# Order and engines of the start-up of a fused Swin block and dynamic convolution on one core: zeroing, bias rows, bias tables and late loads

## The chip, the core and the metric

The kernel runs on one core of a Trainium2 chip. The core has five engines that run their own instruction streams in order: TensorE (PE in the profile; its weight loads are PEld), VectorE (DVE), ScalarE (ACT), GpSimd (POOL) and SyncE (SP), which here only issues transfers. Transfers run on 16 shared DMA engines. TensorE reads SBUF and writes PSUM; PSUM is handed out in four pairs of banks, numbered 0 to 3 in the code.

The metric is device time in microseconds of one execution. The kernel before takes 3045.67 us, the median of three runs (3045.51 to 3046.77).

## What is computed

Two layers on an fp32 tensor x of 16 images, 192 channels, 56 by 56 pixels:

```python
# layer 0: shifted-window attention block, windows of 7x7, 6 heads of 32
h = ln(x, norm1_g, norm1_b)              # over channels, per pixel
h = roll(h, (-3, -3)); win = windows(h)  # 64 windows of 49 tokens per image
q, k, v = split(win @ qkv_w + qkv_b);  q = q * SCALE
attn = softmax(q @ k.T + rel_bias_table + mask)
x1 = x + roll_back(attn @ v @ proj_w + proj_b)
y  = gelu(ln(x1, norm2_g, norm2_b) @ fc1_w + fc1_b) @ fc2_w + fc2_b
x2 = x1 + y
# layer 1: 3x3 depthwise convolution whose taps come from the pooled image
t   = relu(batchnorm(mean(x2) @ w1.T));  taps = (t @ w2.T + b2) * causal_mask
out = depthwise_conv(x2, taps) + bias
```

All runs in one launch; the gains of both normalizations are folded into the weights, and their shifts into the biases.

## The kernel before

**Steps.** One step is seven rows of the upper half and the seven rows 28 further down of one image, that is, 16 windows held as two sets of 8; four steps make an image, 64 steps the batch. `images[b]` holds channels 0 to 127 in one tile and channels 128 to 191 of both halves in another.

**Order.** The schedule is written out by hand: what stands in the code is the order in which each engine gets its instructions (`tc.manual_schedule()`), and each engine executes its own in order. Waits come from data and from the reuse of tiles; tiles that share a tag share a buffer. The loop `for i in range(2, NS + 2)` interleaves the MLP of step i-2, the attention of step i, queries and keys of step i+1 and normalization statistics of step i+2. Ahead of it stand some 250 lines that load parameters and carry steps 0 and 1 through the same stages. The change is there only.

**Normalization.** `norm_stats` forms means of x and of x squared by matmuls with `sel` (tiles `st_a`, `st_b`, `st_c`, then `st`). `norm_vars` takes the squares of the means (ScalarE, L349) and subtracts them (VectorE, L350), `norm_root` takes the root (L354), a VectorE reciprocal of 2.6 us follows. `norm_spread` writes the rows to DRAM and reads them back, each copied to all 128 partitions (`rows`, `dv_*`). Only step 0 takes another way: two matmuls with a column of the identity spread its rows into PSUM (`dv_0`). `norm1_scale` multiplies x by them into windows (`win`, L391 and L399), `norm2_scale` into `yn` (L413 and L419).

**Biases.** `shift` multiplies the norm's shift by the raw weights and copies one row out of PSUM to partition 0 (`qkb_row`, `f1b_row`, L190). `turn_row` turns pieces of that row into columns by matmuls with one row and one column each; VectorE adds them to `qkb`, `bv` (L967) and `f1b` (L1051).

**Operands that must be zero.** Keys go block by block into `kbd` and values into `vbd[0]`, `vbd[1]`, probabilities into `prob[0..3]`; the rest of those tiles stays zero. VectorE clears `kbd` (L922), GpSimd clears `vbd` and `prob` (L997).

**Bias tables.** `biases(r, e)` adds the relative bias and the mask into `bias_t`: six VectorE additions a call (L911). Tables with r = 1 are used by the last step of each image only, first by step 3. All four calls stand in one place, ahead of step 0's scores.

**Attention.** `attention_qk` makes queries and keys (`pq`, `pk`, `pe`), `attention_v` values (`pv`), copied out by `attention_v_out` in two blocks, half by VectorE and half by ScalarE (L524), VectorE first. `attention_scores` gives `sc` and closures `top` (maximum, subtraction, exponential) and `share` (sum, reciprocal, and on GpSimd the product into `prob`, L568). `attention_turn` transposes `prob` (`pt`, copied to `prt`), `attention_values` gives `po`, `project` gives `pp`, and `residual` adds it to x (L651, L657).

**Folded statistics.** `norm_folded` adds both row groups and both channel tiles first: `copies` are two transfers (`xs`), `sums` GpSimd additions (L293, L295), `squares` ScalarE or GpSimd squares (L302, L309, L300), and `fold` two GpSimd additions (L314, L315). The loop's first pass needs those of steps 4 (`1_4`) and 1 (`2_1`) for its matmul `st`, which stands in the middle of `mlp_first` (tile `ph`). Just ahead of the loop:

```python
    copies()
    squares(nc.scalar)()
    table(AF.Gelu)
    sums_((0,))
    yns[0] = norm2_scale(0, dvs.pop(1), True)
    sums_((1,))
    fold()
    attention_v_out(pvs)
```

Of the kernel before, what the change touches and what calls it, by code (L numbers as in the profile page):

```python
# [8 lines left out]
F32 = mybir.dt.float32  # L9
AF = mybir.ActivationFunctionType  # L10
ALU = mybir.AluOpType
AX = mybir.AxisListType

DIM, HEADS, HD = 192, 6, 32
# [22 lines left out]
def tile_swin_then_dynamic_conv(  # L37
# [45 lines left out]
    def banks(name, k):  # L83
        return psum.tile([128, 2, 512], F32, tag=f"pair{k}", name=name)

    def mm(dst, lhs, rhs, start, stop):
        nc.tensor.matmul(dst, lhs, rhs, start=start, stop=stop, skip_group_check=True)  # L87
# [33 lines left out]
    def rows2(dst, src, queue):  # L121

        for h in range(2):
            queue.dma_start(dst[h * 64 : h * 64 + 64], src[C0:DIM])

    def columns_load(sources, tag, name, queue):
        n = sum(count for _, count in sources)
        rows = one.tile([n, 256], F32, tag=tag, name=f"{name}_rows")
        at = 0
        for src, count in sources:  # L130
            queue.dma_start(rows[at : at + count, 0:DIM], src.rearrange("(r c) -> r c", c=DIM))
            at += count
        return rows, n, name
# [37 lines left out]
    def fold_center(dst, n, pm):  # L171
        for c in range(2):
            dv = dst[:, c].rearrange("p (c n) -> p c n", c=2)
            nc.vector.tensor_tensor(dv, dv, pm[:, :, : n // 2], ALU.subtract)
# [17 lines left out]

    def turn_row(dst, row, lo, n):
        mm(dst, row[:, lo : lo + n], ident[0:1, 0:1], True, True)

    ident = const.tile([128, 128], F32, tag="ident", name="ident")
# [7 lines left out]
    wqkv = const.tile([128, 2, 3 * DIM], F32, tag="wqkv", name="wqkv")  # L204
    qkb = const.tile([128, 3], F32, tag="qkb", name="qkb")
    wp0 = const.tile([128, DIM], F32, tag="wp0", name="wp0")
    wp1 = const.tile([128, C0], F32, tag="wp1", name="wp1")
    wp2 = const.tile([128, 128], F32, tag="wp2", name="wp2")
    wf1 = const.tile([128, 2, HID], F32, tag="wf1", name="wf1")
    f1b = const.tile([128, NFC], F32, tag="f1b", name="f1b")  # L210
    wf2 = const.tile([128, NFC, DIM], F32, tag="wf2", name="wf2")

# [25 lines left out]
    rel_r = work.tile([PW, N, HEADS], F32, tag="y", name="rel_r", bufs=3)  # L238
    mask_t = one.tile([PW, 2, 2, N], F32, tag="prt", name="mask_t", bufs=4)

# [102 lines left out]

    def norm_vars(keys, st, tag="dev"):

        lo, hi = min(keys) * 32, max(keys) * 32 + 32
        d = one.tile([128, T], F32, tag=tag, name=f"dev_{keys[min(keys)]}")
        part = d[64 + lo : 64 + hi]
        nc.scalar.activation(part, st[lo:hi, 0, :T], AF.Square)  # L349
        nc.vector.tensor_tensor(part, st[64 + lo : 64 + hi, 0, :T], part, ALU.subtract)  # L350
        return part, d
# [4 lines left out]
    def norm_spread(keys, part, tags=("dv1", "sq01"), order=(1, 0)):  # L356

        rows = dram.tile([2 * len(keys), T], F32, tag="rows", name=f"rows_{keys[min(keys)]}")
        nc.sync.dma_start(rows, part[::16])
        out = {}  # L360
        for side in order:
            if side not in keys:
                continue
            v = one.tile([128, 2, T], F32, tag=tags[side], name=f"dv_{keys[side]}")
            at = 2 * (side - min(keys))
            nc.sync.dma_start(
                v,
                rows[at : at + 2].rearrange("(o h) t -> o h t", o=1).broadcast_to([128, 2, T]),
            )
            out[side] = v  # L370
        return out

# [139 lines left out]

    def attention_v_out(pvs):

        for blk, pv in enumerate(pvs):
            src = pv.rearrange("p h (w n) -> p h w n", w=2)[:, :, :, 0:DIM]
            src = src.rearrange("p h w (g j d) -> p h w g j d", j=2, d=HD)
            for h, copy in enumerate((nc.vector.tensor_copy, nc.scalar.copy)):
                for s in range(2):
                    for j in range(2):  # L520
                        dst = vbd[h][j * 64 : j * 64 + N].rearrange(
                            "p (b w s) g (j d) -> p b w s g j d", b=2, s=2, j=2
                        )[:, blk, :, s, :, j, :]
                        copy(dst, src[s * 64 : s * 64 + N, h, :, :, j, :])  # L524
# [351 lines left out]
    load_rows(*images[0], 0, 2 * WS, 3 * WS, nc.sync)  # L876
    load_rows(*images[0], 0, 3 * WS, HALF, nc.sync)
    nc.sync.dma_start(rawf[:, 0], fc1_w[0:C0])
    rows2(rawf[:, 1], fc1_w, nc.sync)
    nc.vector.memset(wp2, 0.0)  # L880
# [7 lines left out]

    nc.sync.dma_start(mask_t, win_mask)

# [14 lines left out]
    def biases(r, e):  # L905
# [15 lines left out]
    g1, be1, bq, bk, bv = columns(*rows1, 2, nc.vector.tensor_copy)  # L921
    nc.vector.memset(kbd, 0.0)  # L922
    norm_squares("1_0", 0, 0, nc.scalar, ("yn0", "q4"))
    fold_scale(
        raw,
# [12 lines left out]
    norm_stats(keys, {0: 0}, st)  # L938
    part, _ = norm_vars(keys, st, "o")
    norm_root(part)  # L940
    nc.vector.reciprocal(part, part)
    norm_squares("1_1", 1, 0, nc.scalar)
    pm = fold_means(wqkv, 3 * DIM, "fq", 0)
    pq = banks("qkb_p", 2)
    row = shift(pq, raw, 3 * DIM, be1, "qkb_row")
    pq = pq[:, 0, 384:390]
    norm_squares("1_2", 2, 1, nc.scalar)

    pd = banks("dv_0", 3)
    for h in range(2):  # L950
        pick_row = ident[64:96, 64 + h * 16 : 65 + h * 16].broadcast_to([32, 128])
        mm(pd[:, h, :T], pick_row, part, True, True)
    fold_center(wqkv, 3 * DIM, pm)
    parts = (
# [7 lines left out]
    for _, c, at, lo, n, _ in parts:  # L962
        turn_row(pq[at : at + n, c : c + 1], row, lo, n)
    g2, be2, f2b, pb, cb = columns(*rows3, 1, nc.scalar.copy)
    norm1_scale(0, pd[:, :, :T], nc.vector)
    for dst, c, at, _, n, b in parts:
        nc.vector.tensor_tensor(dst, b, pq[at : at + n, c : c + 1], ALU.add)  # L967
    nc.vector.tensor_scalar(qkb[:, 0:1], qkb[:, 0:1], SCALE, None, ALU.mult)
    nc.vector.tensor_scalar(qkb[0:64, 2:3], qkb[0:64, 2:3], SCALE, None, ALU.mult)
    nc.vector.tensor_scalar(kb, pick, qkb[:, 1:2], None, ALU.mult)  # L970


    st = banks("st_b", 0)
    keys = {0: "1_1", 1: "1_2"}
    norm_stats(keys, {0: 1, 1: 2}, st)
    part, _ = norm_vars(keys, st)
    norm_root(part)
# [3 lines left out]
    images[1] = load_x(1, nc.sync)  # L981
    for r in range(2):
        for e in range(2):
            biases(r, e)
    nc.gpsimd.dma_start(wp0, proj_w[0:C0])
# [8 lines left out]
    for k, v in enumerate((running_var, running_mean, gamma, beta)):  # L994
        nc.gpsimd.dma_start(bn[:, k], v.rearrange("(o r) -> o r", o=1).broadcast_to([128, RED]))
    for t in (*vbd, *prob):
        nc.gpsimd.memset(t, 0.0)  # L997

# [9 lines left out]
    norm1_scale(1, dvs.pop(0), nc.gpsimd)  # L1008
    w2v = w2.rearrange("(c t) r -> c t r", t=9)[:, 0:NTAP, :]
    b2v = b2.rearrange("(c t) -> c t", t=9)[:, 0:NTAP]  # L1010
    nc.gpsimd.dma_start(w2n[:, 0], w2v[0:C0])
    nc.gpsimd.dma_start(b2t[:, 0], b2v[0:C0])
    rows2(w2n[:, 1], w2v, nc.gpsimd)
    rows2(b2t[:, 1], b2v, nc.gpsimd)
    nc.gpsimd.dma_start(wf2, fc2_w.rearrange("(f p) n -> p f n", p=128))


    top, share = attention_scores(0, *qs.pop(0), (3, 2, 0, 1))
    pv = banks("pb_p", 3)
    pbp, f1p, pt = pv[:, 0, 384:386], pv[:, 0, 392 : 392 + NFC], pv[:, 1, 384:512]  # L1020
    top(0)
    row = shift(pv, rawf, HID, be2, "f1b_row")

    def rows_to_columns():
        for f in range(NFC):
            turn_row(f1p[:, f : f + 1], row, f * 128, 128)

    qs[1], outs = attention_qk(1, 2, 0, 1, rows_to_columns, nc.vector)

# [17 lines left out]
    share(2)  # L1047
    share(3)
    for c in range(2):
        nc.vector.tensor_tensor(pb[c], pb[c], pbp[:, c : c + 1], ALU.add)  # L1050
    nc.vector.tensor_tensor(f1b, f1b, f1p, ALU.add)  # L1051
    nc.vector.tensor_copy(w1t, pt.rearrange("p (k r) -> p k r", k=2)[:, :, 0:RED])
# [4 lines left out]
    outs[2]()  # L1057
    outs[3]()
    o = attention_rows(0, attention_values(0, prts, 3, 2))

# [14 lines left out]
    norm1_scale(2, dvs.pop(1), nc.gpsimd)  # L1075
    pm = fold_means(wf1, HID, "ff", 1)
    top(2)
    residual(0, pp, pair1)
    norm_squares("2_0", 0, 1, nc.scalar)
# [15 lines left out]
    nc.vector.reciprocal(part, part)  # L1095
    dvs.update(norm_spread(keys, part))
    prts = [attention_turn(1, wp, (2, 0)[wp % 2]) for wp in range(4)]
# [7 lines left out]
    v_rest()  # L1105
    v_whole()
    copies, sums_, squares, fold = norm_folded("1_4", 4, 0)
    copies()
    squares(nc.scalar)()
    table(AF.Gelu)  # L1110
    sums_((0,))
    yns[0] = norm2_scale(0, dvs.pop(1), True)
    sums_((1,))
    fold()
    attention_v_out(pvs)
    pp, pair1, p_narrow, p_rest, p_whole = project(1, o, 3, 2)
# [244 lines left out]
```

## Time and profile before

| part | value | from |
|---|---|---|
| median time | 3045.67 us | the three runs |
| span of the profiled execution | 3044.4 us | page |
| first matmul | 4.17 us | order of time |
| first `pq` (step 0) | 22.55 us | order of time |
| first `po` (step 0) | 53.27 us | order of time |
| first `ph` of the loop | 96.45 us | order of time |
| TensorE busy, windows of 20 us from 0 to 100 | 15.83, 18.61, 19.53, 19.14, 17.54 us | windows |
| DMA share and rate, 0 to 20 us | 0.89, 208 GB/s | windows |

A line in order of time has a start, a duration, the engine, the line of the code, the operation, output and inputs without buffer numbers, a shape, and how often it was merged. In square brackets stands the idle time of the engine before it, and what ended it. A line of the windows view has the stretch, its length, the busy time of PE, PEld, DVE, ACT and POOL with the number of instructions, the clock that TensorE was granted as a share of full speed, the busy share of the DMA engines, and GB/s. A group line of the page has the busy time and the share of the span. Ends of matmuls are modelled, so durations of consecutive matmuls overlap somewhat; starts are the better guide.

### The profile page before, as it was taken

To read this page: it belongs to the slowest core of one execution; us is meant where nothing else is said; L and a number is where in the kernel's file an instruction comes from. 1 tells how busy PE (TensorE), PEld (TensorE's weight loads), DVE (VectorE), ACT (ScalarE), POOL (GpSimd) and SP (SyncE) were. 2 spreads that over 40 slices of the span, in tenths; PEclk is the share of its full clock that TensorE was granted. 3 is DMA by queue.
4 is the path that set the end of the run, shared out by engine and by line. 5 is a ranking of instruction groups with operands and counts; after the bars stand their busy time and mean duration, and the time that the engine had idled before them with its cause. 6 is when DMAs were issued, how large, how long until landed. Compare 5 with 4: busy or idle time off the path is not lost.

```text
span 3044.4 us, 62149 instructions
## 1 busy us (share of the span) xinstructions
PE 3022.7 (99%) x25174; PEld 1891.4 (62%) x25174; DVE 2156.3 (71%) x3841; ACT 1948.7 (64%) x3159; POOL 1343.5 (44%) x1269
## 2 busy tenths in 40 slices
PE   9999999999999999999999999999999999999998
PEld 5666666666666666666666666666666666666654
DVE  8656677676686676776866867767767668668664
ACT  4666676666666666766766667667666667666563
POOL 6444534444435445344444444453454444444422
PEclk9999999999999999999999999999999999999999
DMA  4112121111211112121121211212111121211101
GB/s 111 33 31 59 41 75 41 43 60 46 73 38 62 52 44 68 44 72 36 41 67 47 70 36 52 65 41 78 39 47 56 46 73 38 62 52 43 33 30 56
DMA packets 68711, 159.89 MB, mean 53 GB/s; under 512 B 11250, under 2 KB 35288, under 8 KB 66504
## 3 DMA queue, kind: packets, MB, share of 16 engines
q1 hardware_dynamic: 66766, 153.84, 16.7%
q8 instruction: 199, 3.26, 0.4%
q0 software_dynamic: 1360, 1.26, 0.3%
q14 instruction: 88, 0.72, 0.1%
q10 hardware_dynamic: 298, 0.81, 0.1%
HBM read 92.24 MB, written 38.93 MB: 43 GB/s over the span
## 4 chain that ended last, share of the span: by engine, by line
PE 97%; DVE 1%; DMA 1%; POOL 1%; issue 0%; ACT 0%; SPq 0%; POOLq 0%; DVEq 0%; ACTq 0%
PE ph L87 26%; PE pf L87 25%; PE pv L87 8%; PE pp L87 8%; PE po L87 6%; PE pq L87 5%; PE pt L581 5%; PE sc L87 4%; PE pk L87 4%; PE pe L87 4%; PE st L87 2%; PE pc L87 0%; DMA wp<-in_L_conv_proj_w_dram 0%; PE pb_p L87 0%; DVE e L559 0%
## 5 line engine op out<-in xcount | busy, mean ns | idle before, releaser
L87 PE MATMUL pf<-hid,wf 128*128 128x392 f32 (+1 forms) x3072 | 802.6, 493 | 1.5 <-DVE e L552 1.5
L87 PE MATMUL ph<-yn,wf 128*128 128x392 f32 (+1 forms) x3072 | 799.3, 497 | 1.8 <-ACT vbd L524 1.5
L568 POOL TENSOR_TENSOR prob<-e,tot 113x588 f32<-113x588 f32 x256 | 298.3, 1176 | 1098.8 <-DVE tot L567 1098.6
L87 PEld LDWEIGHTS ph<-yn,wf 128*128 128x128 f32 (+1 forms) x3072 | 426.4, 188 | 346.6 <-issue 47.5
L87 PEld LDWEIGHTS pf<-hid,wf 128*128 128x128 f32 (+1 forms) x3072 | 386.2, 164 | 301.3 <-issue 120.2
L524 ACT COPY vbd<-pv 49x192 f32<-49x192 f32 x512 | 160.5, 313 | 575.9 <-DVE vbd L524 571.4
L717 DVE SCALAR_TENSOR_TENSOR x<-pf,cols,x 128x784 f32<-128x784 f32 (+1 forms) x128 | 106.2, 830 | 506.3 <-PE pf L87 447.6
L671 ACT ACTIVATE hid<-ph,f1b 128x784 f32<-128x784 f32 x384 | 337.2, 913 | 133.7 <-PE ph L87 132.2
L781 DVE SCALAR_TENSOR_TENSOR y<-x,wt,y 128x770 f32<-128x770 f32 x282 | 287.7, 1030 | 15.3 <-ACT y L773 7.0
L87 PEld LDWEIGHTS pv<-wqkv,win 64*128 64x128 f32 (+1 forms) x2048 | 255.4, 188 | 31.4 <-issue 1.2
L87 PE MATMUL pv<-wqkv,win 64*128 64x192 f32 (+1 forms) x2048 | 272.5, 325 | 0.3 <-DVE kbd L470 0.3
L559 DVE TENSOR_TENSOR e<-e,top 113x588 f32<-113x588 f32 x256 | 262.3, 1025 | 8.9
L293 POOL TENSOR_TENSOR xs<-x,x 64x392 f32<-64x392 f32 x246 | 249.1, 1013 | 34.4 <-DVE x L657 25.1
L87 PE MATMUL pp<-o,wp 128*128 128x392 f32 (+2 forms) x896 | 251.4, 514 | 0.0
L587 ACT COPY prt<-pt 128x678 f32<-128x678 f32 x256 | 179.2, 727 | 111.6 <-PE pt L581 110.1
L259 ACT ACT_TABLE_LOAD x192 | 246.3, 1283 | 5.3 <-issue 1.8
L562 ACT ACTIVATE e<-e 113x588 f32<-113x588 f32 x256 | 177.1, 692 | 109.7 <-DVE e L559 109.7
L552 DVE TENSOR_TENSOR e<-sc,bias_t 113x588 f32<-113x588 f32 x256 | 179.5, 762 | 60.6 <-PE sc L87 59.5
L415 POOL TENSOR_TENSOR yn<-x,dv 128x784 f32<-128x784 f32 x62 | 115.8, 1867 | 234.0 <-DMA dv<-rows 234.0
L581 PEld LDWEIGHTS pt<-ident,prob 113*128 113x128 f32 x1536 | 165.4, 141 | 64.9 <-issue 35.1
L87 PE MATMUL po<-prt,vbd 128*64 128x49 f32 x6144 | 196.8, 223 | 0.2 <-ACT prt L587 0.2
L87 PEld LDWEIGHTS po<-prt,vbd 128*64 128x64 f32 x6144 | 188.8, 138 | 9.4 <-ACT prt L587 0.5
(186 smaller groups left out, 4429.3 us busy)
## 6 DMA issues: line engine op xcount, KB each, us to landing
dv<-rows SPq DMA_DIRECT2D x127, 392.0 KB
xs<-x SPq DMA_DIRECT2D x246, 98.0 KB
x<-in_x_dram SPq DMA_DIRECT2D x15, 1484.0 KB
out_dram<-y SPq DMA_DIRECT2D x46, 392.0 KB
out_dram<-y SPq DMA_DIRECT2D x48, 196.0 KB
x<-in_x_dram SPq DMA_DIRECT2D x15, 392.0 KB
x<-in_x_dram SPq DMA_DIRECT2D x15, 350.0 KB
out_dram<-y SPq DMA_DIRECT2D x16, 308.0 KB
```

Of the source, the lines that this page charges most:

```text
L87: nc.tensor.matmul(dst, lhs, rhs, start=start, stop=stop, skip_group_check=True)
L259: nc.scalar.activation(junk, eps_t[0:1], func)
L293: nc.gpsimd.tensor_tensor(xs[p, 0], v0[p, h], v1[p], ALU.add)
L524: copy(dst, src[s * 64 : s * 64 + N, h, :, :, j, :])
L552: nc.vector.tensor_tensor(e, sc[:PW, :, : HEADS * N], rel, ALU.add)
L559: nc.vector.tensor_tensor(ehs[wp], ehs[wp], t.broadcast_to([PW, 2 * HEADS, N]), ALU.subtract)
L562: nc.scalar.activation(es[wp], es[wp], AF.Exp)
L568: nc.gpsimd.tensor_tensor(prob[wp][:PW, :, 0:N], ehs[wp], t.broadcast_to([PW, 2 * HEADS, N]), ALU.mult)
L581: nc.tensor.transpose(pt[:, a, g * PW : (g + 1) * PW], prob[wp][:PW, h : h + 2, :].rearrange("p h k -> p (h k)"), ident[:PW, :PW],)
L587: nc.scalar.copy(prt, pt[:, :, : 3 * PW])
L671: nc.scalar.activation(hid[:, f], phs[f][:, :, :T], AF.Gelu, bias=f1b[:, f : f + 1])
L781: nc.vector.scalar_tensor_tensor(dst, src, wt[:, kc, t : t + 1], dst, ALU.mult, ALU.add)
```

## The change

- The first step's deviations `d0` become a whole tile of 128 rows, zero but for its 32 rows, and both matmuls of `dv_0` run over all 128 rows instead of 32.
- Rows are turned into columns by transfers: six from `qkb_row` into a new tile `pq`, six from `f1b_row` into `f1p`. `turn_row` goes. The second call of `columns` and its TensorE transposes move behind `st_b`.
- A helper `clear` writes zeros by a ScalarE ACTIVATE with scale 0; `kbd` and both `vbd` are cleared so. `prob` is cleared by GpSimd later, behind the second `norm1_scale`.
- Of the bias tables only those with r = 0 are made at the old place; `biases(1, 0)` and `biases(1, 1)` go behind the key copies of steps 1 and 2.
- The loads of `fc1_w` and of x from row 21 on are issued behind the six transfers, the mask ahead of them and into another tag; the loads of `w2`, `b2` and `fc2_w` on GpSimd's queue go behind the first products into `prob`.
- `residual(0)` stands ahead of `top(2)`. The last spread before the loop is read in two parts, the second behind the `xs` copies. The value copies of step 2 are split around `norm2_scale`, and the squares that are left (`rest`) follow them.

It is meant to take small matmuls and waits out of TensorE's way at the start, and to spread the zeroing and the late tables over engines and stretches with room.

```diff
+    def clear(t):
+        names = "abcd"[: len(t.shape) - 1]
+        flat = t.rearrange(f"p {' '.join(names)} -> p ({' '.join(names)})")
+        nc.scalar.activation(flat, ones[:, 0:1].broadcast_to(flat.shape), AF.Copy, scale=0.0)
...
-    def turn_row(dst, row, lo, n):
-        mm(dst, row[:, lo : lo + n], ident[0:1, 0:1], True, True)
...
-    load_rows(*images[0], 0, 3 * WS, HALF, nc.sync)
-    nc.sync.dma_start(rawf[:, 0], fc1_w[0:C0])
-    rows2(rawf[:, 1], fc1_w, nc.sync)
+    nc.sync.dma_start(mask_t, win_mask)
...
-    nc.vector.memset(kbd, 0.0)
+    d0 = one.tile([128, T], F32, tag="o", name="dev_0")
+    nc.vector.memset(d0, 0.0)
     norm_squares("1_0", 0, 0, nc.scalar, ("yn0", "q4"))
+    clear(kbd)
...
-    part, _ = norm_vars(keys, st, "o")
+    part, _ = norm_vars(keys, st, d0)
+    clear(vbd[0])
     norm_root(part)
...
     norm_squares("1_2", 2, 1, nc.scalar)
+    row = shift(banks("qkb_p", 2), raw, 3 * DIM, be1, "qkb_row")
...
-        turn_row(pq[at : at + n, c : c + 1], row, lo, n)
+        nc.sync.dma_start(pq[at : at + n, c : c + 1], row[:, lo : lo + n])
+    nc.sync.dma_start(rawf[:, 0], fc1_w[0:C0])
+    rows2(rawf[:, 1], fc1_w, nc.sync)
+    load_rows(*images[0], 0, 3 * WS, HALF, nc.sync)
...
-        pick_row = ident[64:96, 64 + h * 16 : 65 + h * 16].broadcast_to([32, 128])
-        mm(pd[:, h, :T], pick_row, part, True, True)
+        pick_row = ident[:, 64 + h * 16 : 65 + h * 16].broadcast_to([128, 128])
+        mm(pd[:, h, :T], pick_row, d0, True, True)
     fold_center(wqkv, 3 * DIM, pm)
+    clear(vbd[1])
...
-    for r in range(2):
-        for e in range(2):
-            biases(r, e)
+    for e in range(2):
+        biases(0, e)
...
-    for t in (*vbd, *prob):
-        nc.gpsimd.memset(t, 0.0)
...
+    for t in prob:
+        nc.gpsimd.memset(t, 0.0)
...
-    def rows_to_columns():
-        for f in range(NFC):
-            turn_row(f1p[:, f : f + 1], row, f * 128, 128)
-
-    qs[1], outs = attention_qk(1, 2, 0, 1, rows_to_columns, nc.vector)
+    for f in range(NFC):
+        nc.sync.dma_start(f1p[:, f : f + 1], row[:, f * 128 : (f + 1) * 128])
+    qs[1], outs = attention_qk(1, 2, 0, 1, None, nc.vector)
...
+    biases(1, 0)
+    nc.vector.tensor_tensor(f1b, f1b, f1p, ALU.add)
...
+    residual(0, pp, pair1)
     top(2)
-    residual(0, pp, pair1)
...
-    dvs.update(norm_spread(keys, part))
+    read = norm_spread(keys, part, order=None)
+    dvs[1] = read(1)
...
+    biases(1, 1)
     copies, sums_, squares, fold = norm_folded("1_4", 4, 0)
     copies()
-    squares(nc.scalar)()
+    rest = squares(nc.scalar)
+    sums_((0,))
+    attention_v_out(pvs, (0,))
+    yns[0] = norm2_scale(0, dvs.pop(1), True)
+    dvs[0] = read(0)
+    attention_v_out(pvs, (1,))
+    rest()
     table(AF.Gelu)
-    sums_((0,))
-    yns[0] = norm2_scale(0, dvs.pop(1), True)
     sums_((1,))
     fold()
-    attention_v_out(pvs)
```

## The prediction

> **What bounds the kernel now.** I read the page's busy shares and its chain, then the table by stages, then the order of time of the first 110 us.
>
> ```profile
> PE 3022.7 (99%) x25174; PEld 1891.4 (62%) x25174; DVE 2156.3 (71%) x3841; ACT 1948.7 (64%) x3159; POOL 1343.5 (44%) x1269
> PE 97%; DVE 1%; DMA 1%; POOL 1%; issue 0%; ACT 0%; SPq 0%; POOLq 0%; DVEq 0%; ACTq 0%
> ```
> TensorE is busy 99% of the span and is 97% of the chain. The table of windows (span, then busy time of PE, PEld, DVE, ACT, POOL, granted clock) says where the rest lies:
> ```profile
> 100.00:3020.00 2920.00, 2916.52 (x24349) 1827.64 (x24349) 2062.20 (x3637) 1890.67 (x3057) 1277.46 (x1169) 1.00 0.17 51
> ```
> Between 100 and 3020 us it idles 3.5 us. The change touches only code that runs before 105 us; the order of instructions in the loop is the same. So everything is decided by when TensorE reaches the loop, and by its idle time before 100 us: 9.4 us (the five windows of 20 us have 15.83, 18.61, 19.53, 19.14 and 17.54 busy), 4.2 of which precede its first matmul.
> ```profile
> 17.00:17.50 0.50, 0.50 (x6) 0.43 (x5) 0.27 (x1) 0.46 (x2) 0.50 (x2) 0.60 1.15 218
> 18.50:19.00 0.50, 0.50 (x5) 0.17 (x8) 0.47 (x2) 0.17 (x1) 0.50 (x2) 0.50 0.82 141
> 24.00:24.50 0.50, 0.50 (x6) 0.35 (x4) 0.02 (x1) 0.48 (x2) 0.50 (x1) 1.00 0.54 25
> ```
> The clock column falls to half from 17.4 to 23.9 us. The order of time (start, duration) of that stretch and of the entry to the loop:
> ```profile
> 16.68 1.55 PE L87 MATMUL qkb_p<-ident,qkb_row 1*128 1x1 f32 x9
> 17.23 0.94 DVE L391 TENSOR_TENSOR win<-x,dv 128x343 f32<-128x343 f32 x2 [1.23 <-PE dv L87]
> 19.95 0.38 DVE L399 TENSOR_TENSOR win<-x,dv 64x21 f32<-64x21 f32 x2
> 22.55 1.59 PE L87 MATMUL pq<-win,wqkv 64*128 64x392 f32 x4
> 43.17 1.49 PE L87 MATMUL pb_p<-ident,f1b_row 1*128 1x1 f32 x12
> ...
> 91.00 1.39 POOL L413 TENSOR_TENSOR yn<-x,dv 128x392 f32<-128x392 f32 x1 [10.93 <-DMA dv<-rows]
> 92.66 1.05 ACT L309 ACTIVATE sq<-x 64x392 f32<-64x392 f32 x2
> 94.74 1.01 POOL L314 TENSOR_TENSOR sq<-sq,sq 128x392 f32<-128x392 f32 x1
> 96.45 8.37 PE L87 MATMUL ph<-yn,wf 128*128 128x392 f32 x36 [1.53 <-ACT vbd L524]
> 103.33 1.18 POOL L315 TENSOR_TENSOR sq<-sq 128x392 f32<-128x392 f32 x1
> 104.75 0.11 PEld L87 LDWEIGHTS st<-xs,sel 128*32 128x32 f32 x2 [0.56 <-POOL sq L315]
> ```
> Two waits matter at the end: ph waits 1.5 us for the value copies, and the loop's first st waits for GpSimd's folds, which are done only 0.2 us before it.
>
> [...] half clock after the 1-row matmuls, and again at 3027.4 to 3031 after a pause. [...] on SyncE's queue the trace has 1.7 us (rows issued at 27.11, its reader at 28.82).
>
> **The change part by part.**
> (1) Zeroing. kbd leaves VectorE (2.02 us), d0 comes (392 elements, about 0.35). VectorE gains nothing: its next work waits for qkv_w until 8.79. [...] vbd[0] (1.5 us) starts at 10.56 and holds the root, due 11.21, until 12.0. The reciprocal (2.6) then ends near 15.25 instead of 14.45; dv is queued behind the qkb_p products until 15.54: free, with 0.3 us left. vbd[1] stands behind qkb_row (16.28) and ends at 17.75, before ScalarE's next input. On GpSimd 2.7 us of vbd memsets go; the prob memsets (2.8) move behind the second norm1_scale.
> (2) dv over 128 rows: the same four instructions by 0.33 us. Row count does not lengthen them (fq_m's matmuls on 64 and on 128 rows both come 0.34 apart); [...] I take the clock as kept, and the other end, the full 6.5 us at half rate, for the range.
> (3) Turned rows. The 12 one-row matmuls and the later cols_p leave the way to st_b, which starts near 17.0, not 18.47: 1.5 us. At full clock st_b takes the 2.2 us of st_c (72.17 to 74.3), not 4.1, and ends at 19.2. Then pq waits for win, whose last row starts at 19.95: pq at 20.4 for 22.55 is 2.15 us, and its short part at full clock (2.2 for 2.8, from 111.87 and from 22.55) 0.65 more: **2.8 us** at the first pv. In place of the matmuls VectorE waits for six transfers. They are issued from 16.3, at 0.53 each (rows) until 19.5, landing 1.7 to 2.5 us later: 21.2 to 22. Behind that wait stand qkb, the scales, the second reciprocal (to 25.1), rows and dv_1. q is wanted at 24.2, dv_1 at 30.8: rows lands by 27 and dv_1 about 3 us after its issue, near 30.3. I take it as hidden; 2.5 us a transfer more would show as 1 us.
> (4) Loads. fc1_w (768 KB) and x from row 21 (588 KB) go behind the six transfers. They land near 26; the first reader wants them at 34.
> (5) Bias tables: 6 additions of 0.236 us each are 1.4 us a table. Two leave the stretch before the first vbd copies, which waited for them (32.80, pv ready at 32.4): 0.4 us. One fits into VectorE's 2.6 us wait at 57.1, one into its 3.6 us at 90.9: free. Now 3.2 us ahead.
> (6) The 12 f1b matmuls (43.17 to 44.6) go: 1.4 us, of which ScalarE's kbd ahead of the first prt keeps some 0.8: **3.8 us** ahead. The f1p transfers queue behind image 1, whose traffic ended at 43 and now starts 2 us earlier; they are wanted at 51.
> (7) residual ahead of top(2). ScalarE's e_2 exponential (0.69) now stands ahead of the squares for st_c, which end 0.4 us after pq: 3.4 us ahead at the third pv.
> (8) Last order. dv_0 is read alone, the second dv after the xs copies; dv_0 lands about 4 us after issue (128.28 to 132.19), near 86. VectorE: first vbd half from 86.4 (pv ready 89.7 less 3.4) 1.5, yn 1.4, second half 1.5: 90.9. ScalarE's half 1.3: 92.2, ahead of ph, which starts when pp is done, 94.9-3.4 = 91.5: 4.9 us ahead. But rest() is now behind both copies: squares 0.53+1.05 end at 93.9. GpSimd's chain, two folds, square, sums, add, square, two folds, took 94.74 to 104.51 with 0.5 of wait: 9.3 us. It now starts at 93.9 and ends at 103.2, or 103.9 if norm1_scale on VectorE slows it, as it did the last two folds (1.29, 1.18 for 1.01). TensorE, at st by 99.8, waits 3.5 to 4 us. st starts near 103.5, against 104.75: **1.2 us is kept of 4.9**.
> Sum: 3045.67 - 1.2 = **3044.5**. A pause this long can cost the clock: one window at half rate is 3.4/2 = 1.7 us, which would turn the case into +0.5.
>
> **Rivals.**
> (a) The lead is kept: if GpSimd's folds start earlier than reckoned (copies without waits, TensorE further ahead), all 4.9 us come through, st's 0.3 us too: 3045.67-5.0 = 3040.7. For it: every step before (8) shortens TensorE's own path. Against it: GpSimd executes in order and its folds need ScalarE's last squares.
> (b) Slower: the clock falls at 17 us anyway (st_b then takes 4.1 us and 1.7 us of the lead are lost) or the six transfers hold dv_1 up, and the pause at st still costs 1.7 us of clock: -1.2+1.7+1.7 = +2.2, so 3047.8. For it: 3027 us shows such a fall after a pause of 4 us.
> (c) Much faster, over 6.1 us: all idle time before 96 us gone, with the clock never cold: 5.2 idle + 3.0 matmuls + 3.2 clock = 11.4 at the very most; 3037 if two thirds of it came. The win chain at 17.23 to 20.33 and GpSimd's chain speak against it.
> (d) Much slower: single-word transfers that take 10 us more than reckoned. VectorE's second reciprocal, rows and dv_1 would move by 10, less the 0.5 us of slack at dv_1, and the lead of 1.2 is gone too: 3045.67+9.5-1.2 = 3054.0. Single words on GpSimd's queue (f1b, 3 KB) landed in 5.4 us here; against.
>
> **How the numbers follow.** Main case 0.50, of it a third with a cold window; (a) 0.27; (b) 0.12; (c) 0.07; (d) 0.04. The range must leave out (c), (d) and the outer half of (b), and hold (a): 3040.2 to 3047.5. 0.2% is 6.1 us: only (c) and (d) pass it; with 0.02 and 0.01 more for errors of the working, faster is 0.09, slower 0.05, and 0.86 lies between.
>
> **What would show it.** st_b starting at 17.0 and lasting 2.2 us, clock column 1.00 from 17 to 24; pq at 20.4; pv's sc near 30.6 (33.83 before); po near 49.5 (53.27); ph near 91.5 to 92 without a wait on vbd; then the first st waiting 3 us or more for GpSimd's L315-type fold, at 103 to 104; possibly a half clock behind it. It is wrong if that st starts before 101 (then (a)), if the clock is half at 18 us, or if qkb's additions wait beyond 23 us. A total under 3039.6 or over 3051.8 would mean that something in the loop changed, which I hold to be untouched.

## The result, and the profile after

The kernel after takes **3054.37 us** (median of 6 runs, 3050.24 to 3059.86) against 3045.59 us before (6 runs, 3044.54 to 3047.28): the ratio is 1.003, with an interval of 1.0017 to 1.0043. It is slower by about 9 us, outside the range of 3040.2 to 3047.5. A second set of 18 runs of the same code (`e1_again` below) gave 3051.55 against 3046.24, ratio 1.002 [1.0013, 1.0027]. The profiled execution was the fastest of the first six: its span is 3048.4 us, 4.0 more than before. (A span leaves out about 1.8 us of the device time: this execution took 3050.24 us, the profiled one of before 3046.2.) So two things have to be found: 4 us that the trace holds, and 1 to 5 us that most executions lose on top of it.

The page of the kernel after, the two lines that answer to those of before (busy shares, chain by engine):

```profile
PE 3021.4 (99%) x25150; PEld 1889.3 (62%) x25150; DVE 2160.2 (71%) x3841; ACT 1952.5 (64%) x3162; POOL 1341.1 (44%) x1267
PE 97%; DVE 1%; POOL 1%; DMA 0%; issue 0%; SPq 0%; ACT 0%; POOLq 0%; DVEq 0%
```

They look the same, though TensorE has 24 matmuls and 1.3 us of work less: averages over 3 ms don't show 4 us. The windows do (stretch, length, busy PE, PEld, DVE, ACT, POOL, granted clock):

```profile
17.00:17.50 0.50, 0.50 (x12) 0.26 (x8) 0.50 (x2) 0.27 (x1) 0.50 (x2) 1.00 0.39 66
18.50:19.00 0.50, 0.50 (x9) 0.20 (x2) 0.47 (x4) 0.00 (x0) 0.50 (x2) 1.00 0.06 2
24.00:24.50 0.50, 0.50 (x3) 0.30 (x2) 0.50 (x1) 0.50 (x1) 0.00 (x0) 1.00 1.28 168
100.00:3020.00 2920.00, 2913.37 (x24319) 1824.88 (x24316) 2063.68 (x3631) 1888.39 (x3055) 1278.70 (x1171) 1.00 0.17 51
107.00:110.00 3.00, 3.00 (x5) 1.18 (x4) 0.57 (x1) 0.49 (x1) 0.00 (x0) 0.50 0.00 0
```

The half clock at 17 to 24 us is gone, as intended. In its place stands one from 106.8 to 110.2 us, just behind a pause of TensorE. A stretch at half clock is called cold below, and in the recorded texts also a cold or half-clock window.

The order of time of the first 40 us of the kernel after (start, duration, engine and line; SPq is SyncE's queue of transfers):

```profile
15.91 3.75 SPq L963 DMA_DIRECT2D pq<-qkb_row  x6
16.84 0.94 DVE L398 TENSOR_TENSOR win<-x,dv 128x343 f32<-128x343 f32 x2 [0.83 <-PE dv L87]
19.88 1.04 PE L87 MATMUL pq<-win,wqkv 64*128 64x392 f32 x4 [0.82 <-ACT dev L355]
21.63 0.15 DVE L983 TENSOR_TENSOR cols<-cols,pq 64x1 f32<-64x1 f32 x1 [0.49 <-DMA pq<-qkb_row]
22.07 2.60 DVE L989 RECIPROCAL dev<-dev 64x392 f32<-64x392 f32 x1
22.76 1.71 SPq L112 DMA_DIRECT2D x<-in_x_dram  x1
24.51 1.36 SPq L113 DMA_DIRECT2D x<-in_x_dram  x1
27.49 0.60 SPq L365 DMA_DIRECT2D rows<-dev  x1
29.86 0.80 SPq L370 DMA_DIRECT2D dv<-rows  x2
33.60 1.82 POOL L398 TENSOR_TENSOR win<-x,dv 128x343 f32<-128x343 f32 x2 [12.07 <-DMA dv<-rows]
39.98 1.23 PE L87 MATMUL pq<-win,wqkv 64*128 64x392 f32 x4 [2.08 <-POOL win L406]
```

The first `pq` starts at 19.88 for 22.55, 2.7 us ahead, and the bias additions wait only until 21.63. But the second reciprocal is done at 24.67 and its `rows` transfer is issued at 27.49: SyncE is still issuing loads of x, two of which hold it for 1.71 and 1.36 us. `dv_1` lands at 33.60, GpSimd needs 6.6 us for step 1's windows, and step 1's `pq` waits 2.08 us. It starts at 39.98; before, 40.37. Of a lead of 3.4 us over the trace of before, 0.4 is left.

The entry to the loop of the kernel after, in order of time:

```profile
85.06 0.92 PE L87 MATMUL pv<-wqkv,win 64*128 64x192 f32 x8
88.75 1.46 DVE L532 COPY vbd<-pv 49x192 f32<-49x192 f32 x4 [1.00 <-PE pv L87]
93.69 1.32 ACT L532 COPY vbd<-pv 49x192 f32<-49x192 f32 x4 [2.04 <-DVE vbd L532]
93.69 8.43 PE L87 MATMUL ph<-yn,wf 128*128 128x392 f32 x36
95.47 1.05 ACT L314 ACTIVATE sq<-x 64x392 f32<-64x392 f32 x2
96.60 1.03 POOL L319 TENSOR_TENSOR sq<-sq,sq 128x392 f32<-128x392 f32 x1 [4.92 <-ACT sq L314]
103.39 0.52 PE L87 MATMUL st<-xs,sel 128*32 128x392 f32 x1 [0.50 <-POOL xs L300]
105.50 1.03 POOL L320 TENSOR_TENSOR sq<-sq 128x392 f32<-128x392 f32 x1
106.59 1.38 PE L87 MATMUL st<-sq,sel 128*32 128x392 f32 x2 [2.35 <-POOL sq L320]
113.16 2.24 PE L87 MATMUL sc<-kbd,q 64*64 64x98 f32 x96
```

Two of these points in the kernel before:

```profile
86.14 0.92 PE L87 MATMUL pv<-wqkv,win 64*128 64x192 f32 x8
109.70 2.24 PE L87 MATMUL sc<-kbd,q 64*64 64x98 f32 x96
```

`ph` starts at 93.69 without a wait, 2.8 us earlier than before. Then GpSimd idles 4.92 us for ScalarE's squares, which stand behind both halves of the value copies; its chain of additions and squares runs from 96.60 to 106.53; TensorE waits 0.50 us for the sum `xs`, then 2.35 us, until 106.59, for the last fold, and the clock falls. Step 2's `sc` starts at 113.16 for 109.70: **3.46 us late**. From there to the end only 0.5 us more is lost; the loop carries a lateness on with little added over 2900 us (4.28 us at the tail's first `pc`, 3031.56 for 3027.28).

### The profile page after: what moved, and what is told of

It is laid out like the page before. It is cut to its first block, busy times and chain, and to the rows that moved or that the text cites. A ratio compares the mean times of both kernels' runs of the same rounds, so it can differ in the third digit from the quotient of the medians.

```text
span 3048.4 us, 62116 instructions
## 1 busy us (share of the span) xinstructions
PE 3021.4 (99%) x25150; PEld 1889.3 (62%) x25150; DVE 2160.2 (71%) x3841; ACT 1952.5 (64%) x3162; POOL 1341.1 (44%) x1267
## 4 chain that ended last, share of the span: by engine, by line
PE 97%; DVE 1%; POOL 1%; DMA 0%; issue 0%; SPq 0%; ACT 0%; POOLq 0%; DVEq 0%
PE ph L87 25%; PE pf L87 25%; PE pv L87 8%; PE pp L87 8%; PE po L87 6%; PE pq L87 5%; PE pt L589 5%; PE sc L87 4%; PE pk L87 4%; PE pe L87 4%; PE st L87 2%; PE pc L87 0%; POOL win L406 0%; DVE e L567 0%; POOL win L398 0%
## 5 line engine op out<-in xcount | busy, mean ns | idle before, releaser
L298 POOL TENSOR_TENSOR xs<-x,x 64x392 f32<-64x392 f32 x246 | 249.5, 1014 | 34.5 <-DVE x L665 25.3
```

What stands on the lines that cost most here:

```text
L298: nc.gpsimd.tensor_tensor(xs[p, 0], v0[p, h], v1[p], ALU.add)
```

## The experiments

**Again, and the two suspects taken away.** Four kernels shared one chip and 54 runs of before (3046.24 us). `e1_again` is the kernel after, unchanged.

> The changed kernel once more, for its spread and a second trace. Its six times so far run from 3050.2 to 3059.9 while the kernel before stays within 3044.5 to 3047.3, and the mean granted clock goes down with the time (0.999 at 3048.4 us of span, 0.996 at 3058.1). Theory A (pauses of TensorE before the loop let the clock fall[...]): again 3050 to 3060; in a slow execution the stretches at half clock lie between 17 and 125 us and at the tail, the loop from 140 to 3000 us has its 1.00. Rival B (something in the loop itself got slower, by another layout of SBUF or other transfer lanes): in a slow execution the loss is spread over the loop, each step of about 46 us longer by 0.1 us or more. Rival C (the loop falls to half clock in places): the half-clock stretches lie inside 140 to 3000 us.

Measured: 3051.55 us, 18 runs from 3049.18 to 3057.29. Its profile repeats the pause at the loop's `st`, and has a half clock at a place where the first profile of the same code had none (order of time, then windows):

```profile
39.23 1.98 PE L87 MATMUL pq<-win,wqkv 64*128 64x392 f32 x4 [1.32 <-POOL win L406]
106.32 0.85 PE L87 MATMUL st<-sq,sel 128*32 128x392 f32 x2 [2.35 <-POOL sq L320]
```
```profile
39.00:42.00 3.00, 2.77 (x8) 2.72 (x10) 2.90 (x7) 1.12 (x2) 2.87 (x6) 0.50 0.85 177
107.50:110.50 3.00, 3.00 (x6) 1.42 (x6) 0.57 (x1) 0.62 (x2) 0.00 (x0) 0.50 0.00 0
```

A pause of 1.32 us went with a cold stretch here (from 38.91 us); one of 2.08 us at the same place did not in the first profile. Apart from these two stretches and one behind the pause at the tail, the clock record of this profile, which begins at 8.2 us, has no half clock before the last matmul, so none inside the loop, as theory A has it. None of the longest executions was profiled. But the granted clock of each execution is on record: in the two sets of the kernel after, the seven executions with a mean clock of 0.999 took 3049.18 to 3050.41 us and the three with 0.996 took 3056.43 to 3059.86. A clock lower by 0.003 over 3050 us is an estimated 9.2 us, as far as three decimals tell; that is the size of the scatter. A loop that got slower at full clock (rival B) would not show in that column.

`e2_squares_first` puts the squares ahead of the value copies, and keeps the rest of the change:

```diff
     copies()
-    rest = squares(nc.scalar)
+    squares(nc.scalar)()
...
     attention_v_out(pvs, (1,))
-    rest()
```

> Changed kernel with one part of step 8 undone: the squares of step 4's folded statistics stand ahead of both value copies again, everything else as changed. Theory A (GpSimd's folds wait for ScalarE's last squares, which stand behind the second value copy; TensorE waits at the loop's first st): in the changed kernel's trace the squares end at 96.5 and the chain of folds takes 10.1 us from 96.6. Here the squares can run when the xs copies land, near 88 to 90, and end near 91; GpSimd starts its folds at its own 91.7 and ends near 101.5; TensorE, at st by 101.9, waits less than 0.5 us; no clock fall there. About 3.5 us for the wait and 1.5 us for the clock less: 3045 or less in its fastest execution, and a spread as small as that of the kernel before if this pause causes the spread. Rival B (another GpSimd or VectorE wait takes its place, residual or the transfers of 2_1): st still starts after 104, at most 1.5 us gained.

Measured: 3045.57 us, ratio 0.9997 [0.9989, 1.0005]. One moved statement is worth 6.0 us (3051.55 less 3045.57), and takes the whole loss away. What is left of the change, steps (1) to (7) of the prediction and the rest of (8), is not told apart from before. In order of time:

```profile
89.73 1.05 ACT L314 ACTIVATE sq<-x 64x392 f32<-64x392 f32 x2
92.15 1.33 POOL L319 TENSOR_TENSOR sq<-sq,sq 128x392 f32<-128x392 f32 x1
101.57 1.17 POOL L320 TENSOR_TENSOR sq<-sq 128x392 f32<-128x392 f32 x1
102.54 0.53 PE L87 MATMUL st<-xs,sel 128*32 128x392 f32 x2
```

The squares end at 90.8 instead of 96.5, GpSimd's last fold at 102.74, and `st` no longer waits.

`e3_x_later` issues x from row 21 on behind the spread of step 1's deviations, so that SyncE is free for `rows`:

```diff
-    load_rows(*images[0], 0, 3 * WS, HALF, nc.sync)
...
     dvs.update(norm_spread(keys, part, tags=("dv1", "yn0"), order=(0, 1)))
+    load_rows(*images[0], 0, 3 * WS, HALF, nc.sync)
     images[1] = load_x(1, nc.sync)
```

> Changed kernel with one load moved: x from row 21 on is issued behind rows and the two dv reads instead of ahead of them. Theory A (SyncE is still issuing that load when the reciprocal is done at 24.7, so rows goes out at 27.5 and dv_1 lands at 33.6; GpSimd's windows and with them TensorE's second pq wait 2.1 us): rows goes out near 24.8, dv_1 lands near 30.5, the second pq starts near 37.9 instead of 39.98, and po of step 0 near 49.5 instead of 51.1. Since the wait at st follows ScalarE and VectorE, which follow TensorE, st also comes about 1.5 us earlier: 1 to 2 us less in all. Rival B (dv_1 is late because of the transfers' own traffic, fc1_w and image 1, not because of the issue order): rows earlier but dv_1 still near 33, no gain.

Measured: 3051.67 us, ratio 1.0017 [1.001, 1.0024], the same as `e1_again`. In order of time:

```profile
30.92 1.82 POOL L398 TENSOR_TENSOR win<-x,dv 128x343 f32<-128x343 f32 x2 [9.54 <-DMA dv<-rows]
37.23 1.00 PE L87 MATMUL pq<-win,wqkv 64*128 64x392 f32 x4
67.94 1.79 PE L87 MATMUL pq<-win,wqkv 64*128 64x392 f32 x4 [1.01 <-POOL win L406]
```
```profile
68.00:72.00 4.00, 4.00 (x20) 1.33 (x24) 3.93 (x7) 1.74 (x3) 1.37 (x2) 0.57 0.00 0
```

The cause of the first wait is shown: with the loads out of the way `dv_1` lands at 30.92 for 33.60 and `pq` of step 1 starts at 37.23 without a wait. The forecast of 1 to 2 us in all fails, as the gain does not last. Step 2's `pq` now comes early enough to wait 1.01 us for GpSimd's `win`, the clock falls behind it in this execution, and the pause at the loop's `st` (106.23, again 2.35 us) is there in any case.

`e4_both` joins the two edits.

> Both edits of the two runs before together. Theory A (the two waits are the whole of the loss): second pq near 37.9, ph near 91 to 92, st without a long wait near 100; about 3041, under the kernel before by 4 to 5 us, with a small spread. Rival B (one of the waits hid another): over 3044. Rival C (the spread is not due to pauses): the time scatters by 5 us and more as that of the changed kernel does.

Measured: 3045.40 us, ratio 0.9996 [0.9988, 1.0004]; not told apart from before, nor from `e2_squares_first`. Theory A's 3041 is missed by over 4 us, and rival B's "over 3044" holds: the two waits are not all. In its profile step 3's first `pq` starts 2.9 us earlier than before (108.99 for 111.87), but the span is only 0.7 us shorter: 0.9 of the lead goes in the loop and 1.3 in the last 100 us.

**The order alone, and the pause filled.** The next four shared a chip and 65 runs of before (3046.77 us). `e5_order_alone` is the kernel before with step 8 of the prediction and nothing else:

```diff
...
-    dvs.update(norm_spread(keys, part))
+    read = norm_spread(keys, part, order=None)
+    dvs[1] = read(1)
...
-    squares(nc.scalar)()
-    table(AF.Gelu)
+    rest = squares(nc.scalar)
     sums_((0,))
+    attention_v_out(pvs, (0,))
     yns[0] = norm2_scale(0, dvs.pop(1), True)
+    dvs[0] = read(0)
+    attention_v_out(pvs, (1,))
+    rest()
+    table(AF.Gelu)
     sums_((1,))
     fold()
-    attention_v_out(pvs)
```

> The kernel before with the last step's order alone (own squares behind both value copies, dv_0 read apart). Theory A, the wait at the loop's first st is the loss: pv ready 89.7, VectorE's half copy to 91.2, yn 92.6, second half 94.1, ScalarE's half 95.4, squares end 96.9, GpSimd's chain 9.9 us, so st's last part at 106.8 instead of 104.75; with one half-clock window behind it the first pq of step 3 at 115.5 instead of 111.9, and the time 3049.5 to 3050.5 against 3046. Theory B, the loss comes from the early part (load order, pauses at 40 us): this order gains the 1 us of ph's wait and the time is 3045 to 3046.

Measured: 3052.34 us, ratio 1.0015 [1.0009, 1.0022]: +5.6 us, where the whole change gave +5.3 in `e1_again`. The order is sufficient by itself. That is 2 us more than theory A's 3049.5 to 3050.5; the cold stretch behind the pause lasts 6.83 us here, two times 3.41. In order of time, with the lines as the kernel before numbers them (its L309, L314 and L315 are L314, L319 and L320 above), and the windows:

```profile
95.05 1.05 ACT L309 ACTIVATE sq<-x 64x392 f32<-64x392 f32 x2
96.18 1.03 POOL L314 TENSOR_TENSOR sq<-sq,sq 128x392 f32<-128x392 f32 x1 [3.62 <-ACT sq L309]
106.17 1.51 PE L87 MATMUL st<-sq,sel 128*32 128x392 f32 x2 [2.35 <-POOL sq L315]
```
```profile
17.00:17.50 0.50, 0.50 (x8) 0.36 (x6) 0.20 (x1) 0.50 (x2) 0.50 (x2) 1.00 1.14 227
100.00:120.00 20.00, 17.15 (x145) 8.52 (x142) 12.01 (x20) 8.65 (x12) 5.88 (x6) 0.83 0.05 11
```

The second fence holds a surprise: this kernel has the one-row matmuls and the 32-row `dv` of before, and its clock at 17 us is full. The fall in the profile of before (at 17.10 us by the clock record; the prediction read 17.4) is not in every execution. That changes how the lead has to be read, since up to 82 us this kernel does what before does (each column is one execution):

| | before | `e5_order_alone` | after |
|---|---|---|---|
| cold at 17 us | 6.83 us | none | none |
| start of the first `pq` | 22.55 | 20.34 | 19.88 |
| start of step 0's `sc` | 33.83 | 31.15 | 30.61 |
| start of step 0's `po` | 53.27 | 51.50 | 51.13 |
| start of step 2's `pv` | 86.14 | 84.34 | 85.06 |

At the first `pq` 2.2 of the 2.7 us that the kernel after gains over the trace of before are gained by the old code as well when its clock stays full, and at step 2's `pv` the kernel after is 0.72 us behind it.

`e6_fill_st` is the kernel after with three extra products ahead of the last `st` product:

```diff
         for k, at in order:
+            if folded and at == 3 and "1_4" in keys.values():
+                for _ in range(3):
+                    mm(st[:, 1, :T], ident, wqkv[:, 0, 0:T], True, True)
```

> The kernel after, with three extra products of 128x392 (about 0.70 us each) put into the unused second bank of the loop's first st tile ahead of its last product; nothing reads them. They fill 2.1 of the 2.4 us that TensorE waits there. Theory A, wait and clock are two separate losses: last st product still near 106.5, granted clock 1.00 from 100 to 120 us, first pq of step 3 near 113.5 (115.1 in the kernel after, 111.9 before), profiled span near 3046.8, and the median falls from 3051.5 by 1.7 (one window) to 3.4 (two windows). Theory B, the slower executions lose their clock elsewhere: the median stays within 1 us of 3051.

Measured: 3050.76 us, ratio 1.0011 [1.0005, 1.0018], +4.0 against its runs of before where `e1_again` had +5.3. The profile:

```profile
105.87 2.24 PE L87 MATMUL st<-wqkv,ident 128*128 128x392 f32 x6
108.29 0.84 PE L87 MATMUL st<-sq,sel 128*32 128x392 f32 x2 [0.19 <-POOL sq L320]
```
```profile
106.50:110.00 3.50, 3.31 (x10) 1.36 (x9) 2.41 (x7) 0.49 (x1) 1.66 (x2) 1.00 0.10 23
```

The clock holds behind `st`, as theory A has it; its other numbers fail. This execution was cold at 39.5 us and once more at 70.2, and so came to 108.29 late, and the median lies within 1 us of 3051, which was theory B's number, not 1.7 to 3.4 us lower. The 1.3 us between the two differences is too small for its intervals to settle. So the trace shows that the pause need not cost the clock, and the median gives no sign that this pause alone makes the slower executions.

`e7_narrow_dv` is `e4_both` with `dv` on 32 rows:

```diff
-        pick_row = ident[:, 64 + h * 16 : 65 + h * 16].broadcast_to([128, 128])
-        mm(pd[:, h, :T], pick_row, d0, True, True)
+        pick_row = ident[64:96, 64 + h * 16 : 65 + h * 16].broadcast_to([32, 128])
+        mm(pd[:, h, :T], pick_row, part, True, True)
```

> e4_both with the first deviations again on 32 rows (dv's products contract over 32 rows). Theory A, the small number of rows is what let the clock fall at 17 us before: half clock from 16 to 20.5 us or to 24, st_b 3.5 to 4 us long instead of 2.1, first sc at 32 to 33 instead of 30.8, time 1.7 us above e4_both: near 3047. Theory B, the one-row products were the reason, and they are gone here: clock 1.00 at 17 us, first sc at 30.8, time equal to e4_both: 3045.4.

Measured: 3045.50 us, ratio 0.9994 [0.9986, 1.0002], as `e4_both`; clock 1.00 from 17 to 18 us, first `sc` at 30.77 (30.83 in `e4_both`). Theory B's numbers; the zeroed 128-row tile did nothing that can be measured. That the one-row products were the reason does not follow: `e5_order_alone` has them too, and its clock held. One trace can't exclude that the clock would fall here in other executions.

**The pauses filled everywhere.** `e8_fills` is `e4_both` with extra products ahead of step 1's and step 2's `pq` and ahead of the tail's first `pc`, where TensorE waits 3.09 us for GpSimd in before and after alike:

```diff
+        if i in (1, 2):
+            mm(ps[0][:, 0, :T], ident, wqkv[:, 0, 0:T], True, True)
         for m in (0, 2, 1):
             short(dsts[m], wqkv, slice(m * 128, (m + 1) * 128), r1, True)
...
         pc = banks(f"pc_{n}", k)
+        for _ in range(0 if n else 4):
+            mm(pc[:, 0, :T], ident, wqkv[:, 0, 0:T], True, True)
```

> e4_both with extra products that nothing reads (128x392, 0.70 us each): one ahead of the first pq of steps 1 and 2, four ahead of the first pc at the tail, each in a bank that is overwritten next. Theory A, half-clock windows follow from pauses: no half window at 40, 70 or behind pc; pc's 32 products take about 10.7 us instead of 12.4, profiled span near 3042, median 3042.5 to 3043.5. Theory B, the pauses do not set the clock: half windows stay, and the time is 3045.4 or a little above.

Measured: **3043.61 us**, ratio 0.9989 [0.9982, 0.9995]: faster than both kernels, and 0.1 above theory A's range. Its clock has no half stretch from 10.8 us until behind its last matmul. Its tail, and below it that of the kernel after:

```profile
3021.16 2.87 PE L87 MATMUL pc<-wqkv,ident 128*128 128x392 f32 x8
3024.42 10.66 PE L87 MATMUL pc<-x,dg 128*128 128x392 f32 x32 [0.40 <-POOL dg L1287]
```
```profile
3031.56 12.35 PE L87 MATMUL pc<-x,dg 128*128 128x392 f32 x32 [3.09 <-POOL dg L1284]
```

The 32 products of `pc` take 10.66 us for 12.35: 2.9 us of work for nothing buys 1.7 us.

`e9_before_tail` is the kernel before with the four products ahead of `pc` alone, `e10_after_fills` the kernel after with its waits left in and filled: two products at step 1's `pq`, one at step 2's, three at `st`, four at `pc`. They shared 25 runs of before (3046.24 us).

> The kernel before with the four extra products of 128x392 ahead of the first pc alone (they fill the 3.1 us pause at the tail; nothing reads them). If the cold window behind that pause costs what e8_fills showed (pc 10.66 us long instead of 12.4 to 13.2, which is 1.7 to 2.5 us), the median falls from 3046.5 to 3044 to 3045, and what e8_fills keeps beyond this (3043.6) is what the mended change is worth: 0.5 to 1.5 us. If the gain of e8_fills came from the early part, this stays at 3046 to 3046.5.

Measured: 3044.69 us, ratio 0.9996 [0.9987, 1.0004]; its profile has `pc` at 10.66 us, and was cold for 3.41 us from 17.44 on. By the medians about half of what `e8_fills` gained is the tail; the rest, some 1.6 us against before (3.16 less 1.55), is what the mended change and the two small fills are worth, and the intervals overlap.

> The kernel after with extra products that nothing reads at each pause: two ahead of pq of step 1, one ahead of pq of step 2, three ahead of the last st product at the loop's entry, four ahead of the first pc. Its waits stay. Theory A, the slower executions of the kernel after (up to 8 us above its fastest) are cold windows behind these pauses: clock 1.00 throughout, last st still near 106.5, median 3046 to 3047.5, and the runs lie within 4 us. Theory B, the clock falls elsewhere too: median 3049 or more, and the runs spread over 6 us or more as before.

Measured: 3047.67 us, ratio 1.0005 [0.9997, 1.0013], 13 runs from 3046.61 to 3049.05: a spread of 2.4 us, where the 18 runs of `e1_again` have 8.1. The waits are where they were, and the clock is full from its first record, at 7.8 us, on; before that the view counts as full what is not recorded, though equal products take longer there (up to 0.86 us in `st_a`, 0.49 to 0.52 in `st_b`, in the kernel after). In order of time, then windows:

```profile
106.60 0.84 PE L87 MATMUL st<-sq,sel 128*32 128x392 f32 x2 [0.18 <-POOL sq L320]
111.52 2.24 PE L87 MATMUL sc<-kbd,q 64*64 64x98 f32 x96
```
```profile
0.00:110.00 110.00, 99.95 (x806) 59.73 (x807) 90.08 (x199) 60.56 (x102) 65.40 (x98) 1.00 0.36 90
110.00:3020.00 2910.00, 2906.21 (x24295) 1822.56 (x24294) 2055.31 (x3619) 1885.46 (x3051) 1272.27 (x1165) 1.00 0.17 51
```

Its last `st` starts at 106.60 as in the kernel after (106.59), and step 2's `sc` at 111.52, not 113.16. So of the 3.46 us there, 1.64 are clock and 1.82 are what the wait costs beyond the lead. And its median lies 1.43 us above before, not 5.3 to 8.8: the slower executions of the kernel after were cold stretches behind pauses. The fill at the tail helps before as well: against `e9_before_tail`, which has it too, the median is 2.98 us longer. The median is 0.2 us above the interval that theory A gave; its other numbers hold.

## Why the prediction was wrong

The steps up to the first scores hold within 0.6 us. Zeroing on ScalarE (1) cost nothing (2.15 us for `kbd`, 1.48 for each `vbd`); `st_b` started at 16.67 (17.0 forecast) and took 2.1 us at full clock (2.2); `pq` at 19.88 (20.4), step 0's `sc` at 30.61 (30.6), the six transfers landed by 21.6 (21.2 to 22), 2.0 us behind the end of their issue. That the whole tile would keep the clock (2) was the author's estimate; no run shows it, and in `e7_narrow_dv` the clock is 1.00 from 17 to 18 us with 32 rows. What loses the time is the order of step (8), by `e2_squares_first` and `e5_order_alone`; the forecast missed it by three wrong terms and by the clock.

**Steps (3) and (4): "I take it as hidden".** `dv_1` was put near 30.3 and landed at 33.60. The transfers of single words were sized rightly, and so was `rows` as far as the reciprocal goes (24.67 for 25.1). What was missed is SyncE's queue itself. Step (4) asked when the loads' bytes land, not how long their issue holds the queue: from 19.7 to 27.0 us. `e3_x_later` shows it: there `rows` is issued at 24.57 in place of 27.49. The lead at the third `pv` (step 2's), put at 3.4 us, measured 1.08 (85.06 for 86.14).

**Step (5), a small one.** Six additions for one table were put at 1.4 us; they took 2.75 at 52.36, beside GpSimd's squares, and step 1's last scores started at 57.52 after 0.82 us of idle time for which the profile names no releaser ("issue"). `e5_order_alone`, which has the tables at the old place, has no stop there: all 96 products of that `sc` in one run of 2.61 us from 54.43. Part of the 1.2 us that the lead shrank between step 0's `po` (51.13 for 53.27) and step 1's `pv` (57.83 for 58.78) is this; it was not tried by itself.

**Step (8): the term mis-sized, the mechanism right.** The wait was named: the squares behind both copies, GpSimd's chain, TensorE stopping at `st`. From values ready to the last `st` the prediction had 17.2 us (86.3 to 103.5), the trace 17.8 (88.75 to 106.59); the chain took 9.9 us for 9.3, stretched where it ran beside VectorE's `win` (L298 2.53 us; 2.09 in `e2_squares_first`, where it ran at 95.80 and `win` began at 99.43). The tables show the like from the other side: the second one's six additions took 1.48 us at 86.27, beside an idle GpSimd, where the first took 2.75. So 2.3 us of the 3.1 at `st` are the lead that was not there, and 0.6 the chain.

The error in reasoning is to have set the lead against the wait. By the prediction's own numbers and with no lead, the last `st` comes at 89.7 + 17.2 = 106.9, 2.2 us behind the 104.75 of before; the lead of 3.4 was to pay for that. But the chain starts from the same values as TensorE's path to `st` and moves with them, so the order costs the same with any lead, and should have been judged without one. From the start of step 2's `pv` to the end of the last wait at `st` TensorE takes 21.5 us in the kernel after, in `e1_again`, `e3_x_later` and `e6_fill_st` and 21.8 in `e5_order_alone`, with that `pv` anywhere from 84.34 to 86.75, against 18.6 before and 17.0 in `e2_squares_first`. (That the pause itself is 2.35 us each time says less: TensorE already waits for `xs` there, 0.5 us in all four, and only three GpSimd instructions follow.)

**The clock.** "A pause this long can cost the clock ... +0.5" was right in kind: 1.64 us of the 1.7 reckoned, half of a stretch of 3.4 us (it lasted 3.41, as did the one behind the pause at the tail of before). It was held to be a third of one case; all four profiles with the unfilled pause at `st` show it. In sum: -1.2 forecast, +2.3 lead, +0.6 chain, +1.6 clock give +3.3, where the trace has +3.46 at step 2's `sc` and +4.0 at the end.

**What no step had: the executions that are not profiled.** The prediction worked from one trace of before to one trace of after. Cold stretches behind the pauses differ between executions: the median lies above the profiled execution's own time by 4.1 us in the first set of the kernel after (3054.37, 3050.24) and by 1.3 in `e1_again` (3051.55, 3050.30), by nothing for before (3046.24, 3046.2) or `e10_after_fills` (3047.67, 3047.93). Why the two sets of the same code differ by 2.8 us is open. And most of the forecast lead of step (3), 2.8 us, counted on a fall of the clock that before has in two of three profiles of that code (before, `e9_before_tail`; not `e5_order_alone`). In the table above, with the clock full on both sides, steps (1) to (7) bring 0.5 us at the first `pq` and have lost it at step 2's `pv`. Even with x issued later, in `e4_both`, whose clock held there too, that `pv` starts at 84.03, only 0.3 us ahead of `e5_order_alone`.

Of the rivals, (b) comes nearest: the pause costs clock and `dv_1` is held up. It had the transfers at fault in place of the queue behind them, and was given a chance of 0.12. That the first set's 3054.37 all but equals the 3054.0 of (d) is chance: the single words landed when forecast, by 21.6 us. (Two sums there are off: two thirds of 11.4 us would be 3038, not 3037, in (c), and (d) takes the lead as gone and still subtracts it.) Last, a total over 3051.8 was to mean that something in the loop had changed. It does not: the loop adds 0.8 us to the lateness in 2900 us, and the slower executions are those with the lower granted clock.

## What to carry to other kernels

Before moving a producer behind other work, follow both paths from their last common input to the place where they meet: only the difference of their lengths counts, and a lead won earlier shifts both. When a queue gets more transfers, price the time of each issue and look for the small, urgent one behind them. Where the bound engine has short pauses behind which its clock falls in some executions (here behind one of 1.32 us in `e1_again`, not behind one of 2.08 us at the same place in the kernel after), compare distributions and the clock column, not two single traces, and don't book as a gain what one execution lost to its clock; filling a pause with products that nothing reads can be cheaper than the pause (2.9 us of them for a gain of 1.7 at the tail of `e8_fills`).

## What the runs showed of the hardware

- **The clock's stretches come in units.** In the clock records of these traces every half-clock stretch before the last matmul lasts 3.41 or 6.83 us, and two in one execution start a whole number of units of 3.4133 us apart (106.76 and 3031.98 in the kernel after: 2925.22 us, 857 units; 17.10 and 3027.66 in before: 3010.56 us, 882 units). The first record of full clock starts at 7.77 us in the kernel after and at 10.27 in before. How busy TensorE was in the unit just before does not decide whether the clock falls: at step 1's `pq` the unit with most of the pause was busy 1.94 us in the kernel after (38.49 to 41.91) and the clock held, and busy 2.42 us in `e1_again` (35.50 to 38.91) and it fell.
- **The clock also fell behind a busy unit.** At 17.10 us in before it fell after a unit in which TensorE was busy all 3.41 us. The prediction ties that fall to the one-row products; `e5_order_alone` has them too, from 16.41, and its clock is full at 17.0 to 19.0. Busy time as the trace shows it doesn't tell which units lead to a fall; what does stays open.
- **SyncE's issue time varies.** Six transfers of one column each took 3.75 us to issue, 0.62 each; loads of x rows took 0.47 to 0.59 us and, between 22.76 and 25.87, 1.71 and 1.36. Behind the transfers of `norm_spread`, in `e3_x_later`, the same six loads of x took 0.42 to 0.59. What lengthened the two is not shown.
